# Heads of two tiles at a time, block sums accumulated in PSUM, hid times dt on ScalarE, and the norm's sums by transposes

## The chip, the cores and the metric

The kernel runs on one core of a Trainium2 chip. The metric is the device time of one execution in microseconds. Before the change it is 859.09 us, the median of 3 runs (858.77 to 859.28).

## The reference

One decoder layer in fp32 on x of 2 batches x 256 tokens x 512 channels. Its first part, a state-space block, is where nearly all the time goes:

```
h    = rmsnorm(layernorm(x)) * norm_w
proj = h @ in_proj_w.T                  # gate 8192 | hid 8192, B 1024, C 1024 | dt 128
hBC  = silu(causal_conv(hBC, conv_w) + conv_b)       # 4 taps along the tokens
dt   = softplus(dt + dt_bias);  A = -exp(A_log)
# 128 heads of 64 channels, 8 groups of 16 heads; chunks of 128 tokens
L    = exp(segsum(A * dt))                           # decay between tokens
y    = ((C B^T) * L) @ (hid * dt)  + state of the chunk before + Dp * hid
yg   = y * silu(gate)
y    = yg * rsqrt(mean over each group of 1024 channels of yg^2 + 1e-5) * gnorm_w
x    = x + layernorm(x) + y @ out_proj_w.T
```

Then follow a product of fake-quantised rows with a fake-quantised context, and a feed-forward part with a low-rank mix of experts; they are the last 60 us or so.

## The kernel before

The 512 tokens lie side by side (T = 512, two batches of S = 256). The 8192 channels are 64 tiles of 128 channels, two heads each. Eight tiles make a group g (0 to 7). The main loop (L979 to L1074) is a software pipeline over steps: step s begins tile z, goes on with z1 (begun a step before) and ends z2 (two before). A group has nine steps, q = 0 to 8: eight tiles and, at q = 4, the B and C channels of the next group ("State"; the last group has none and so has eight steps). The order of the instructions on TensorE, VectorE, ScalarE and GpSimd is the order of the program text; only the DMA queue on SP is ordered by the scheduler.

A step does the following.

- `begin(z)` projects the tile's gate and hid rows. In group 0 and for the first tile of group 1 ("plain") this is eight products of 512 columns. Later a scheme with seven block products instead of eight is used (Strassen's): a block product is two matmuls of 128x128 by 256 columns. `begin` issues four of them, `complete` three. In between, ScalarE copies one product to SBUF (`copy_first`, L387), VectorE forms sums (`sum_begun`, L395 to L397), and after `complete` VectorE adds what is saved (`sum_complete`, L410, L411). `sum_weights` on GpSimd forms the sums of the weights (L352 to L355) for the next step's tile.
- `start_conv` and `Conv.finish`: the first tap with the bias on ScalarE (L313), three taps on VectorE (L318), silu on ScalarE (L321). `gates` makes silu of the gate.
- `decayed` and `weighted` for both heads: a scan on VectorE (L493), two multiplies on ScalarE (L497), and GpSimd's product with C B^T (`inner`), called mT (L503).
- `seventh`: the output projection of the group before, also in seven blocks m1 to m7 of eight matmuls with 256 columns (L637). Which block runs at which q is in `usual`; m2 and m4 are split over two steps (q = 2 and 3, q = 8 and 0). Before them GpSimd forms sums of yw and wo (`usual_sums`, L584 to L612). m6, at q = 4, needs the sums of L590 and L604, made at q = 3.
- `heads(z2)`: eight matmuls of 64 weight columns for the tile's two heads, which fill two halves of the array (L513). `gated`: VectorE adds the skip term and multiplies by the gate (L525, L528), ScalarE squares (L533) and scales (L535), GpSimd adds up the squares (L534).
- `by_tokens(z1)`: four transposes of hid on TensorE into the bank "misc" (L477), and on VectorE hid times dt for the heads (L481, called hc).
- `norm(outs[g - 1])` at q = 2: four matmuls of the summed squares with a column of ones (L542), VectorE (L546), then the inverse root on GpSimd (L41 to L51).

On TensorE the order within a step is: `begin`, C B^T or the norm where they are due, block, heads, transposes, `complete`. A matmul in fp32 is two records in the trace, a transpose one. PSUM's eight banks: "py" (heads), "misc", "seed", "po" (blocks), and four for the projection, as two buffers of two banks.

Of the kernel before, what the change touches and what calls it, by code (L numbers as in the profile page):

```python
# [14 lines left out]
NB = 2  # L15
# [39 lines left out]
def kernel(  # L55
# [40 lines left out]
    ramp = const.tile([P, P], F32, name="ramp")  # L96
# [36 lines left out]
    nc.vector.tensor_tensor_scan(ramp[:], ones[:], ones[:], 0.0, ALU.mult, ALU.add)  # L133
    rowno = ps_misc.tile([P, P], F32, tag="misc", name="rowno")
    nc.tensor.matmul(rowno[:], ramp[0:1, :], ones[0:1, :], start=True, stop=True)
    nc.vector.tensor_tensor(ident[:], rowno[:], ramp[:], ALU.is_equal)
# [5 lines left out]
    with ExitStack() as first:  # L142
# [22 lines left out]
        for b in range(NB):  # L165
# [5 lines left out]
            if b == 0:  # L171
                halves = [
                    ps.tile([P, 2, S], F32, tag=tag, name=f"pt_0_{tag}")[:]
                    for ps, tag in ((ps_misc, "misc"), (ps_y, "py"))
                ]
            else:
                halves = [
                    ps_proj.tile([P, 2, T], F32, tag="xy", name=f"pt_1_{h}")[:, 0, :].rearrange("p (k s) -> p k s", k=2)
                    for h in range(2)
                ]  # L180
# [115 lines left out]
    def multiply(out, w, h):  # L296
        for k in range(KD // 2):
            nc.tensor.matmul(out, w[:, k, :], h[:, k, :], start=(k == 0), stop=(k == KD // 2 - 1))  # L298
# [59 lines left out]
    def begin(z):  # L358

        if isinstance(z, State) and z.plain:  # L360

            c = ps_out.tile([P, T], F32, tag="po", name=f"c_{z.g}")
            if z.g == 0:
                b = ps_misc.tile([P, T], F32, tag="misc", name="b_0")
                z.xy = [b[:], c[:]]
            else:
                xy = ps_proj.tile([P, 2, T], F32, tag="xy", name=f"b_{z.g}")
                z.xy = [xy[:, 0, :], c[:]]
        else:
            xy = ps_proj.tile([P, 2, T], F32, tag="xy", name=f"xy_{z.name}")  # L370
            z.xy = [xy[:, n, :] for n in range(2)]
            z.flat = xy[:].rearrange("p n s -> p (n s)")
        if z.plain:
            for n in range(2):
                project(z.xy[n], z.w[:, n])
            return
        z.halves = [z.xy[n][:, half] for n in range(2) for half in (slice(0, S), slice(S, T))]
        x0, x1, y0, y1 = z.halves
        multiply(x0, z.a11, h00)
        multiply(x1, z.s2, t2)  # L380
        multiply(y0, z.s1, t1)
        multiply(y1, z.s3, t3)

    def copy_first(z):
        if not z.plain:
            z.u = pool.tile([P, 2, S], F32, tag="u", name=f"u_{z.name}")
            nc.scalar.copy(z.u[:, 0], z.halves[0])  # L387

    def sum_begun(z):
        if not z.plain:  # L390
            z.v = pool.tile([P, 2, S], F32, tag="v", name=f"v_{z.name}", bufs=1)
            _, x1, _, y1 = z.halves
            u0, u1 = z.u[:, 0], z.u[:, 1]
            y = by_batch(z.xy[1])
            nc.vector.tensor_tensor(u1, x1, u0, ALU.subtract)  # L395
            nc.vector.tensor_tensor(z.v[:], y, z.u[:, 1:2].to_broadcast([P, 2, S]), ALU.subtract)
            nc.vector.tensor_tensor(u1, z.v[:, 0], y1, ALU.add)  # L397

    def complete(z):
        if not z.plain:  # L400
            _, x1, y0, y1 = z.halves
            multiply(x1, z.a12, h10)
            multiply(y0, z.s4, h11)
            multiply(y1, z.a22, t4)

    def sum_complete(z):
        if not z.plain:
            x1 = z.halves[1]
            y = by_batch(z.xy[1])
            nc.vector.tensor_tensor(x1, x1, z.u[:, 0], ALU.add)  # L410
            nc.vector.tensor_tensor(y, y, z.v[:], ALU.add)  # L411

    def hid_of(z):
        return by_batch(z.xy[0] if z.plain else z.flat[:, S : S + T])

    def start_conv(z):
        if isinstance(z, Tile):
            z.hid = pool.tile([P, T], F32, tag="hid", name=f"hid_{z.c}", bufs=2)
            z.convs = [Conv(z.hid[:], [hid_of(z)], cw[:, z.c], z.c, f"h_{z.c}")]
# [3 lines left out]
        z.convs = [Conv(z.sT[0][:], [hid_of(z)], cw[:, 64 + g], 64 + g, f"b_{g}")]  # L423
        if z.plain:
            pvs, w = [by_batch(z.xy[1])], cw[:, 72 + g]
        else:

            pvs, w = [a.unsqueeze(1) for a in (z.halves[3], z.u[:, 1])], ncw[:, g]
        z.convs.append(Conv(z.sT[1][:], pvs, w, 72 + g, f"c_{g}"))

    def gates(z, half):
        if half == 0:
            z.gate = pool.tile([P, T], F32, tag="gate", name=f"gate_{z.c}", bufs=2)
        cols = slice(half * S, (half + 1) * S)
        if not z.plain:

            nc.scalar.activation(z.gate[:, cols], (z.halves[3], z.u[:, 1])[half], AF.Silu, scale=-1.0)
# [34 lines left out]
    def by_tokens(z):  # L472

        c = z.c
        pht = ps_misc.tile([P, NT, 2, HD], F32, tag="misc", name=f"pht_{c}")
        for t in range(NT):
            nc.tensor.transpose(  # L477
                pht[:, t].rearrange("p h d -> p (h d)"), z.hid[:, t * P : (t + 1) * P], ident[:]
            )
        z.hc = pool.tile([P, NT, 2, HD], F32, tag="hc", name=f"hc_{c}", bufs=2)  # L480
        nc.vector.tensor_tensor(  # L481
            z.hc[:],
            pht[:],
            dt[:, :, 2 * c : 2 * c + 2].unsqueeze(3).to_broadcast([P, NT, 2, HD]),
            ALU.mult,
        )

    def decayed(z, n):
# [3 lines left out]
        lT = pool.tile([P, NT + NB, P], F32, tag="lT", name=f"lT_{z.c}_{n}", bufs=4)  # L492
# [7 lines left out]
    def weighted(z, n, inner):  # L500

        m = pool.tile([P, NT + NB, P], F32, tag="mT", name=f"mT_{z.c}_{n}", bufs=4)
# [3 lines left out]
    def heads(z):  # L506

        z.py = ps_y.tile([P, T], F32, tag="py", name=f"py_{z.c}")
# [12 lines left out]
    def gated(z, sqsum, yw):  # L521
# [9 lines left out]
        else:  # L531
            sq = pool.tile([P, T], F32, tag="sq", name=f"sq_{c}", bufs=1)
# [4 lines left out]
    def norm(o):  # L537

        g = o.g
        pss = ps_misc.tile([P, NT], F32, tag="misc", name=f"pss_{g}")  # L540
        for t in range(NT):
            nc.tensor.matmul(  # L542
                pss[:, t : t + 1], o.sqsum[:, t * P : (t + 1) * P], ones[:, 0:1], start=True, stop=True
            )
        var = small.tile([P, NT], F32, tag="var", name=f"var_{g}")
        nc.vector.tensor_scalar(var[:], pss[:], 1.0 / (GJ * P), 1e-5, ALU.mult, ALU.add)  # L546
# [206 lines left out]
    class Rows:  # L753
# [17 lines left out]
        def scaled(self, name, scale):  # L771
# [10 lines left out]
            self.x = pool.tile([P, D], F32, tag="hid", name=f"x_{name}_{t}", bufs=2)  # L782
# [118 lines left out]
    def experts(lo):  # L901
# [21 lines left out]
        for t in range(NT):  # L923
            pf = rows[t].pf
            out_t = pool.tile([P, D], F32, tag="lT", name=f"out_{t}", bufs=4)
# [10 lines left out]
    def finish(z):  # L936
        g, j = divmod(z.c, GJ)
        o = outs[g]
        heads(z)
        if j == 0:  # L940
            o.sqsum = pool.tile([P, T], F32, tag="sqsum", name=f"sqsum_{g}", bufs=1)
        if j % 2 == 0:
            new_yw(o)
        gated(z, o.sqsum, o.yw[-1][:, j % 2, :])
# [26 lines left out]

    sum_inputs()
# [6 lines left out]
    for s, (g, q, z) in enumerate(order):  # L979
# [8 lines left out]
        if z1:  # L988
            sum_complete(z1)
# [7 lines left out]
        if z1:  # L997
            start_conv(z1)
        if tile1:
# [14 lines left out]
        if q == 2 and 0 < g < NG:  # L1014
            norm(outs[g - 1])
        if z:
            sum_begun(z)
        if z1 and not tile1:
            z1.convs[1].finish()
            state = z1  # L1020
        for o, turn in ((outs[g] if g < NG else None, q - GT), (outs[g - 1], q)):
# [21 lines left out]
        o = outs[g - 1]  # L1043
        if not going and 0 <= o.g < g and not o.plain and q in turns[o.g]:
            going.append(seventh(o, *turns[o.g][q]))
# [17 lines left out]
        if isinstance(z2, Tile):  # L1063
            finish(z2)
        if tile1:
            by_tokens(z1)
        if z:
            complete(z)
        if 2 <= s < 2 + 2 + NT:
# [125 lines left out]
```

## Time and profile before

| | |
|---|---|
| median of 3 runs | 859.09 us (858.77 to 859.28) |
| the profiled execution | 858.99 us, span 856.5 us |
| granted TensorE clock | 0.998 |
| busy: TensorE, VectorE, GpSimd, ScalarE | 849.2, 725.5, 655.5, 365.1 us |
| DMA | 116.21 MB, mean 136 GB/s |
| TensorE and GpSimd from 319.93 to 417.52 us (nine steps) | 97.47 and 86.63 of 97.59 us |
| mean of one: L481, L396, L410, L411 (VectorE) | 681, 692, 430, 699 ns |
| mean of one: L387, L497, L535 (ScalarE) | 372, 395, 706 ns |
| mean of one: L503, L534 (GpSimd) | 1819, 1283 ns |

The span is from the first to the last instruction of the profiled execution; what lies around it (2.5 us here) is in the run's time but not in the span. A row of the timeline has its start, its length, the engine, the line, what is written from what, the shape, and how many instructions are merged in it. Matmuls overlap in their pipeline, so their lengths add up to more than the time that passes; from the start of one row to the start of the next is what passes.

### The profile page before, as it was taken

The page shows a single profiled execution, that of the slowest core. Times are in us where ns is not written, and L with a number is a line of the kernel's source. Part 1 is how long each engine was busy: PE and PEld are TensorE (multiplying, and loading weights), DVE is VectorE, ACT ScalarE, POOL GpSimd, SP SyncE. Part 2 cuts the span into 40 slices and gives each one's busy share as a digit, 9 for nine tenths or more (in the row PEclk, how much of TensorE's full clock was granted, in tenths as well). Part 3 has the DMA queues.
Part 4 walks back from the last instruction along what each step waited for, and adds up shares of the span by engine and source line. Part 5 has one row for each costly group of instructions (what it writes and reads, how often), then busy time and mean ns, then how long its engine had stood idle before and what let it go on. Part 6 is the DMA issues. An engine that isn't in the chain of part 4 may idle for free.

```text
span 856.5 us, 13149 instructions
## 1 busy us (share of the span) xinstructions
PE 849.2 (99%) x4432; PEld 655.2 (76%) x4432; DVE 725.5 (85%) x1146; ACT 365.1 (43%) x791; POOL 655.5 (77%) x674
## 2 busy tenths in 40 slices
PE   9999999999999999999999999999999999999998
PEld 6444588888888888888888888888888888885453
DVE  5788699899989899899989899899899898995663
ACT  2444554444544544435443444434443444443220
POOL 2156789988899779997899789997899789973210
PEclk9999999999999999999999999999999999999999
DMA  5774463237542483235632374235433363323001
GB/s 173 221 292 129 128 184 126 81 110 225 171 122 86 124 269 125 86 123 183 212 123 86 116 223 130 75 111 189 161 122 91 118 222 106 123 86 124 0 1 49
DMA packets 54419, 116.21 MB, mean 136 GB/s; under 512 B 7217, under 2 KB 7473, under 8 KB 54354
## 3 DMA queue, kind: packets, MB, share of 16 engines
q1 hardware_dynamic: 54354, 115.39, 42.0%
q8 instruction: 35, 0.57, 0.3%
q14 instruction: 30, 0.25, 0.1%
HBM read 111.83 MB, written 3.54 MB: 135 GB/s over the span
## 4 chain that ended last, share of the span: by engine, by line
PE 90%; DVE 6%; issue 1%; DMA 1%; ACT 1%; SPq 0%; ACTq 0%
PE xy L298 35%; PE m L637 18%; PE py L513 10%; PE xy L294 7%; PE xy_bc L298 4%; PE pht L477 4%; PE po L694 3%; DVE conv_h L318 2%; PE pf L803 2%; PE pq L803 2%; DVE lT L493 1%; PE pcb L446 1%; PE b L294 1%; PE c L294 1%; PE pss L542 1%
## 5 line engine op out<-in xcount | busy, mean ns | idle before, releaser
L503 POOL TENSOR_TENSOR mT<-lT,inner 128x768 f32<-128x768 f32 x128 | 232.7, 1819 | 91.6 <-ACT lT L497 89.0
L493 DVE TENSOR_TENSOR_SCAN lT<-dec,seed 128x512 f32<-128x512 f32 x128 | 154.9, 1211 | 0.0
L637 PE MATMUL m<-wo,yw 128*128 128x256 f32 x672 | 154.6, 380 | 0.0
L318 DVE SCALAR_TENSOR_TENSOR conv_h<-xy,cw,conv_h 128x510 f32<-128x510 f32 (+2 forms) x192 | 143.0, 745 | 13.0 <-ACT gate L439 4.9
L637 PEld LDWEIGHTS m<-wo,yw 128*128 128x128 f32 x672 | 125.9, 190 | 16.8 <-POOL wo L604 0.7
L497 ACT ACTIVATE lT<-dec,lT 128x128 f32<-128x128 f32 x256 | 88.6, 395 | 115.4 <-DVE lT L493 109.5
L298 PE MATMUL xy<-hT,w 128*128 128x256 f32 x440 | 114.1, 382 | 0.5
L298 PE MATMUL xy<-hs,w 128*128 128x256 f32 x440 | 112.9, 379 | 0.0
L298 PE MATMUL xy<-hs,ws 128*128 128x256 f32 x440 | 103.9, 379 | 0.0
L513 PE MATMUL py<-mT,hc 128*64 128x256 f32 (+1 forms) x1024 | 97.3, 332 | 0.0
L534 POOL TENSOR_TENSOR sqsum<-sqsum,sq 128x512 f32<-128x512 f32 x56 | 71.9, 1283 | 33.0 <-ACT sq L533 33.0
L513 PEld LDWEIGHTS py<-mT,hc 128*64 128x64 f32 x1024 | 63.4, 136 | 42.3 <-issue 19.8
L298 PEld LDWEIGHTS xy<-hs,w 128*128 128x128 f32 x440 | 83.6, 190 | 11.4
L298 PEld LDWEIGHTS xy<-hs,ws 128*128 128x128 f32 x440 | 83.6, 190 | 11.4
L298 PEld LDWEIGHTS xy<-hT,w 128*128 128x128 f32 x440 | 79.2, 190 | 11.0 <-DVE u L397 1.5
L313 ACT ACTIVATE conv_h<-xy,cb,cw 128x512 f32<-128x512 f32 x64 | 49.6, 775 | 62.9 <-DVE xy L411 62.6
L533 ACT ACTIVATE sq<-y 128x512 f32<-128x512 f32 x56 | 35.3, 630 | 95.0 <-DVE y L528 95.0
L525 DVE SCALAR_TENSOR_TENSOR py<-hid,dsk,py 128x512 f32<-128x512 f32 x64 | 47.8, 746 | 19.1 <-PE py L513 18.5
L294 PE MATMUL xy<-hT,w 128*128 128x512 f32 x144 | 63.4, 593 | 0.0
L298 PE MATMUL xy<-hT,ws 128*128 128x256 f32 x220 | 56.5, 379 | 0.0
L321 ACT ACTIVATE hid<-conv_h 128x512 f32<-128x512 f32 x64 | 40.2, 628 | 29.5 <-DVE conv_h L318 29.1
L294 PEld LDWEIGHTS xy<-hT,w 128*128 128x128 f32 x144 | 26.7, 190 | 30.4 <-issue 29.4
(230 smaller groups left out, 1395.0 us busy)
## 6 DMA issues: line engine op xcount, KB each, us to landing
dec<-decays SPq DMA_DIRECT2D x128, 384.0 KB, 3.5
w<-in_in_w SPq DMA_DIRECT2D x128, 256.0 KB, 3.0
wo<-in_out_w SPq DMA_DIRECT2D x16, 1024.0 KB, 6.0
w_bc<-in_in_w SPq DMA_DIRECT2D x16, 256.0 KB, 3.2
kvin<-in_ctx_kv SPq DMA_DIRECT2D x4, 512.0 KB, 4.0
kvq<-kvin SPq DMA_DIRECT2D x4, 512.0 KB, 5.3
kv<-kvq SPq DMA_DIRECT2D x4, 512.0 KB, 3.6
acc<-in_x SPq DMA_DIRECT2D x4, 256.0 KB, 3.5
```

Of the source, the lines that this page charges most:

```text
L294: nc.tensor.matmul(pp, w[:, k, :], hT[:, k, :], start=(k == 0), stop=(k == KD - 1))
L298: nc.tensor.matmul(out, w[:, k, :], h[:, k, :], start=(k == 0), stop=(k == KD // 2 - 1))
L313: nc.scalar.activation(a, pv, AF.Identity, bias=cb[:, c : c + 1], scale=w[:, 3:4])
L318: nc.vector.scalar_tensor_tensor(a[:, :, d:], pv[:, :, : S - d], self.w[:, 3 - d : 4 - d], a[:, :, d:], ALU.mult, ALU.add)
L321: nc.scalar.activation(self.dst, self.a[:], AF.Silu)
L493: nc.vector.tensor_tensor_scan(lT[:, 0:NT, :].rearrange("p t i -> p (t i)"), dec[:, 0:T], seed[:], 0.0, ALU.mult, ALU.add)
L497: nc.scalar.mul(lT[:, NT + b, :], dec[:, T + b * P : T + (b + 1) * P], lT[:, 2 * b, P - 1 : P])
L503: nc.gpsimd.tensor_tensor(m[:], z.lT[n][:], inner[:], ALU.mult)
L513: nc.tensor.matmul(z.py[n * HD : (n + 1) * HD, b * S + s * P : (b + 1) * S], z.hc[:, 2 * b + s, n, :], z.mT[n][:, part, :], start=(s == 0) ...
L525: nc.vector.scalar_tensor_tensor(py[:], hid[:], dsk[:, c : c + 1], py[:], ALU.mult, ALU.add)
L534: nc.gpsimd.tensor_tensor(sqsum[:], sqsum[:], sq[:], ALU.add)
L637: nc.tensor.matmul(o.po[:, t, :], lhs[k][:, t * P : (t + 1) * P], rhs[k], start=(k == 0), stop=(k == GJ // 2 - 1))
```

## The change

Heads. `finish` takes a list: tiles are gathered until there are two (or one, in group 0 and at q = 0 and 1), then the heads of both are issued one after the other and after that both are gated. An even tile's result goes to bank "py", an odd one's to "misc". The transposes of z1 come after `complete` and go to whichever of the two banks is given (`free`). hid and gate get three buffers, mT six, sq two; lT three instead of four.

hid times dt. At the next step's start, ahead of `gates` and `copy_first`, ScalarE multiplies the transposed values by dt, for each token tile and head: eight instructions of 128x64 instead of VectorE's one of 128x512.

Block sums. The two projection banks of a tile are allocated apart ("x" and "y"). `begin` writes four block products in another order and place, `copy_first` copies two of them, VectorE makes four sums of 256 columns, partly in PSUM itself, and `complete` adds its three block products to what is in PSUM by accumulation (only the first product that writes a bank clears it). `sum_complete` is gone.

Norm. Four transposes of the summed squares into "py", then a VectorE reduction along the free axis; `norm` is called after `sum_begun`.

Also, the ramp that makes the identity shares its buffer, and the condition that starts a block of `seventh` is written otherwise, with the same blocks at the same steps.

```diff
-    def multiply(out, w, h):
+    def multiply(out, w, h, clear=False):
         for k in range(KD // 2):
-            nc.tensor.matmul(out, w[:, k, :], h[:, k, :], start=(k == 0), stop=(k == KD // 2 - 1))
+            nc.tensor.matmul(out, w[:, k, :], h[:, k, :], start=clear and k == 0, stop=(k == KD // 2 - 1), skip_group_check=True)
...
-        z.halves = [z.xy[n][:, half] for n in range(2) for half in (slice(0, S), slice(S, T))]
-        x0, x1, y0, y1 = z.halves
-        multiply(x0, z.a11, h00)
-        multiply(x1, z.s2, t2)
-        multiply(y0, z.s1, t1)
-        multiply(y1, z.s3, t3)
+        z.h0, z.h1, z.g0, z.all = (z.xy[n][:, half] for n in range(2) for half in (slice(0, S), slice(S, T)))
+        multiply(z.g0, z.s3, t3, clear=True)
+        multiply(z.all, z.s2, t2)
+        multiply(z.h0, z.a11, h00, clear=True)
+        multiply(z.h1, z.s1, t1)
...
-            z.u = pool.tile([P, 2, S], F32, tag="u", name=f"u_{z.name}")
-            nc.scalar.copy(z.u[:, 0], z.halves[0])
+            z.first = pool.tile([P, 2, S], F32, tag="first", name=f"first_{z.name}", bufs=1)
+            nc.scalar.copy(z.first[:, 1], z.g0)
+            nc.scalar.copy(z.first[:, 0], z.h0)
...
-            nc.vector.tensor_tensor(u1, x1, u0, ALU.subtract)
-            nc.vector.tensor_tensor(z.v[:], y, z.u[:, 1:2].to_broadcast([P, 2, S]), ALU.subtract)
-            nc.vector.tensor_tensor(u1, z.v[:, 0], y1, ALU.add)
+            z.g1 = pool.tile([P, S], F32, tag="g1", name=f"g1_{z.name}")[:]
+            u = z.first[:, 0]
+            nc.vector.tensor_tensor(u, z.all, u, ALU.subtract)
+            nc.vector.tensor_tensor(z.h1, z.h1, u, ALU.subtract)
+            nc.vector.tensor_tensor(z.g1, z.h1, z.first[:, 1], ALU.add)
+            nc.vector.tensor_tensor(z.g0, z.g0, u, ALU.subtract)
...
-            multiply(x1, z.a12, h10)
-            multiply(y0, z.s4, h11)
-            multiply(y1, z.a22, t4)
-
-    def sum_complete(z):
-        if not z.plain:
-            x1 = z.halves[1]
-            y = by_batch(z.xy[1])
-            nc.vector.tensor_tensor(x1, x1, z.u[:, 0], ALU.add)
-            nc.vector.tensor_tensor(y, y, z.v[:], ALU.add)
+            multiply(z.h0, z.a12, h10)
+            multiply(z.h1, z.s4, h11)
+            multiply(z.g0, z.a22, t4)
...
-    def by_tokens(z):
+    def by_tokens(z, bank):
...
+        ps, tag = ((ps_misc, "misc"), (ps_y, "py"))[bank]
+        pht = ps.tile([P, NT, 2, HD], F32, tag=tag, name=f"pht_{c}")
...
+    def times_dt(z):
+        c, pht = z.c, z.pht
         z.hc = pool.tile([P, NT, 2, HD], F32, tag="hc", name=f"hc_{c}", bufs=2)
-        nc.vector.tensor_tensor(
-            z.hc[:],
-            pht[:],
-            dt[:, :, 2 * c : 2 * c + 2].unsqueeze(3).to_broadcast([P, NT, 2, HD]),
-            ALU.mult,
-        )
+        for t in range(NT):
+            for n in range(2):
+                h = 2 * c + n
+                nc.scalar.mul(z.hc[:, t, n], pht[:, t, n], dt[:, t, h : h + 1])
...
-            nc.tensor.matmul(
-                pss[:, t : t + 1], o.sqsum[:, t * P : (t + 1) * P], ones[:, 0:1], start=True, stop=True
-            )
+            nc.tensor.transpose(pss[:, t, :], o.sqsum[:, t * P : (t + 1) * P], ident[:])
         var = small.tile([P, NT], F32, tag="var", name=f"var_{g}")
-        nc.vector.tensor_scalar(var[:], pss[:], 1.0 / (GJ * P), 1e-5, ALU.mult, ALU.add)
+        nc.vector.tensor_reduce(var[:], pss[:], AX.X, ALU.add)
+        nc.vector.tensor_scalar(var[:], var[:], 1.0 / (GJ * P), 1e-5, ALU.mult, ALU.add)
...
-    def finish(z):
+    def finish(pair):
+
+        for z in pair:
+            heads(z)
+        for z in pair:
...
-        if z1:
-            sum_complete(z1)
...
+        if isinstance(z2, Tile):
+            times_dt(z2)
...
-        if not going and 0 <= o.g < g and not o.plain and q in turns[o.g]:
-            going.append(seventh(o, *turns[o.g][q]))
+        for n in (1, 2):
+            turn = q + (n - 1) * GT
+            if 0 <= g - n < NG - 1 and turn in turns[g - n]:
+                going.append(seventh(outs[g - n], *turns[g - n][turn]))
...
-            finish(z2)
-        if tile1:
-            by_tokens(z1)
+            pair.append(z2)
+
+        done = len(pair) == 2 or len(pair) == 1 and (q < 2 or g == 0)
+        free = 0
+        if done:
+            free = 1 - len(pair) % 2 * (1 - pair[0].c % 2)
+            finish(pair)
+            pair = []
         if z:
             complete(z)
+        if tile1:
+            by_tokens(z1, free)
```

## Prediction before the run

> **What bounds the kernel now.** I read the page's busy times, then the chain that ended last, then the timeline of TensorE, start to start, and last VectorE, ScalarE and GpSimd in the same window.
>
> ```profile
> PE 849.2 (99%) x4432; PEld 655.2 (76%) x4432; DVE 725.5 (85%) x1146; ACT 365.1 (43%) x791; POOL 655.5 (77%) x674
> ...
> PE 90%; DVE 6%; issue 1%; DMA 1%; ACT 1%; SPq 0%; ACTq 0%
> ```
>
> TensorE is in use all the time and carries 90% of the chain. But a busy TensorE can still stand between instructions, so I read its timeline by the distance from one row's start to the next row's start.
>
> ```profile
> 410.59 0.66 PE L477 MATMUL pht<-ident,hid 128*128 128x128 f32 x4
> 411.37 1.13 PE L298 MATMUL xy<-hT,w 128*128 128x256 f32 x4
> 412.34 1.03 PE L298 MATMUL xy<-hT,ws 128*128 128x256 f32 x4
> 413.20 1.03 PE L298 MATMUL xy<-hs,w 128*128 128x256 f32 x4
> ...
> 417.52 0.95 PE L542 MATMUL pss<-ones,sqsum 128*128 128x1 f32 x8
> 418.33 1.97 PE L637 MATMUL m<-wo,yw 128*128 128x256 f32 x8
> 420.23 1.52 PE L513 MATMUL py<-mT,hc 128*64 128x256 f32 x16
> 421.69 0.66 PE L477 MATMUL pht<-ident,hid 128*128 128x128 f32 x4
> 422.18 1.03 PE L298 MATMUL xy<-hT,w 128*128 128x256 f32 x4
> 423.04 1.03 PE L298 MATMUL xy<-hT,ws 128*128 128x256 f32 x4
> ```
>
> Four records of a 256-column product take 0.86 to 0.87 us (412.34 to 413.20), so 0.216 us each; that is the flow. Against it: (a) eight L637 records should take 1.73 us and take 1.90 (418.33 to 420.23): 0.08 after the one-column products of L542, 0.09 on entering the heads. (b) The heads (L513) take 1.46 us. Their eight matmuls are two records each, and two heads flow side by side, so 1.30 us is flow; 0.05 is lost behind the first pair and 0.09 on leaving. (c) The transposes take 0.49 us, against 4 x 0.109 = 0.44 when nothing precedes them. So a run of heads with transposes behind it costs 0.09 + 0.05 + 0.09 + 0.06 = 0.29 us beside its flow. With a full product behind it (the next rows) that product's first four records take 0.97 instead of 0.87: 0.34 us.
>
> ```profile
> 355.56 1.52 PE L513 MATMUL py<-mT,hc 128*64 128x256 f32 x16
> 357.01 1.13 PE L298 MATMUL xy<-hT,w 128*128 128x256 f32 x4
> 357.98 1.03 PE L298 MATMUL xy<-hT,ws 128*128 128x256 f32 x4
> ```
>
> (d) At 410.59 the transposes are followed only at 411.37, 0.78 later: TensorE waits for VectorE's u (L397). This pause of 0.39 us comes four times (118, 216, 313 and 411 us), always in q = 1 of a group in which VectorE also quantises the context (L269, L270). (e) The last tight place is GpSimd's:
>
> ```profile
> 419.11 1.82 POOL L503 TENSOR_TENSOR mT<-lT,inner 128x768 f32<-128x768 f32 x1
> ...
> 436.28 2.49 POOL L604 TENSOR_TENSOR wo<-wo,t 128x512 f32<-128x512 f32 x2
> ```
>
> ```profile
> 438.04 3.65 PE L637 MATMUL m<-wo,yw 128*128 128x256 f32 x16
> ```
>
> Between these GpSimd has no gap. The block m6 starts at 438.04 and needs the second L604 result, done at 438.77, from its third product on, at 438.9: nothing is to spare. If TensorE comes earlier there, it waits.
>
> **The change, part by part.** Times are within one step of the loop, t = 0 at TensorE's first projection product.
>
> Pairs of heads. The instruction order of the changed kernel has 43 runs of heads instead of 64: group 0 singly, then per group three pairs and two singles. The transposes move behind the products that complete the projection. Before: 56 runs with transposes behind at 0.29 and 8 with a product behind at 0.34, 19.3 us with unrounded sums (0.295, 0.343). After: 7 and 36, 14.4 us. Gain 4.9 us, all on TensorE. What is delayed: the first tile of a pair comes one step later; its buffers (hid, gate three, mT six) cover that, and its py, pht and hc buffers are read at least a step before they are wanted again.
>
> Norm. Eight one-column records (0.81 + 0.08 us) become four transposes (0.44): 0.45 us, seven times on the path, 3.2 us. The Trainium skill speaks against it: "TensorE: Matmul & The Clock Gate", Part 4: PE-mode transpose, gives about 275 ns for a transpose within a kernel; four would be 1.10 us, and the seven norms would lose 1.5 us. The row here has 0.109 us from start to start for just this form, so I take the gain. VectorE gets a reduction of 128x512 (nearest row L481, 0.68) ahead of L546, so the scale comes about 0.5 us later. In the last norm TensorE gains 0.45 while add_out starts 0.4 later, with other products between: I count -0.2 (from -0.5 to +0.4).
>
> Block sums in PSUM. VectorE drops L396, L410 and L411 (0.69 + 0.43 + 0.70) and issues two more of 0.42: -0.97 us for each of 61 tiles. With hc (0.68 x 64) gone and the reductions added, VectorE goes from 725 to about 628 us. TensorE's products stay as many. The only part of this on the path is (d): the sums are then done at about t = 5.8 in q = 1 (context 0.9, scan 1.2, convolution 2.3, three sums 1.35), and the completing products want them at 6.91 + 1.55 = 8.4. Gain 4 x 0.39 = 1.5 us. Without this cover it stays at nothing.
>
> hid times dt on ScalarE, and one more copy (0.37). The trace has no 128x64 multiply from PSUM.
>
> ```profile
> L497 ACT ACTIVATE lT<-dec,lT 128x128 f32<-128x128 f32 x256 | 88.6, 395 | 115.4 <-DVE lT L493 109.5 <-DMA dec<-decays 5.9
> ...
> L387 ACT COPY u<-xy 128x256 f32<-128x256 f32 x55 | 20.5, 372 | 52.7 <-PE xy L298 52.6
> ...
> L194 ACT ACTIVATE hT<-pt,nw 128x256 f32<-128x256 f32 x2 | 0.8, 471 | 0.1
> ```
>
> Two multiplies follow each other at 0.31 us with 128 columns (L497) and at 0.37 with 256 (L194, which reads PSUM). At the 0.83 ns per column between the 512- and 256-column copies, 64 columns give 0.25 and 0.21; I take 0.24, bounds 0.21 and 0.31. Eight are 1.9 us a tile; ScalarE goes from 365 to about 510 us. They stand ahead of the two copies and of L497 in ScalarE's queue, and for those wait VectorE's sums, the completing products and GpSimd's mT. In most steps this is hidden: the second copy cannot start before t = 3.7 (417.77 - 414.07 in the trace: all four products have to end), and convolution 0.6, eight multiplies to 2.5, gate and first copy to 3.25 are through by then. The copy ends at 4.07, three sums at 5.5. The completing products want them at 5.6 in q = 2 (projection 3.46, norm 0.44, half a block 1.73), at 6.7 in q = 0, at 6.9 in q = 4 and 6, later elsewhere. So cover is thin, and three places get a wait:
> - m6 in q = 4. From q = 2's start TensorE needs 8.65 + 11.15 + 3.46 = 23.3 us to m6 (before: 438.04 - 414.07 = 23.97). GpSimd's stretch of 19.66 us (419.11 to 438.77) starts at 4.8, not 5.04, because mT waits for L497, that for the second copy; perhaps 0.2 goes to the later norm. It ends at 24.5 to 24.7; the third product wants it at 24.15. Wait 0.3 to 0.5 and 0.1 to restart: 0.5 us in 6 groups, 3.0 us (0 to 4).
> - q = 0 with the context's Relu (L267, 1.23 us) at the head of ScalarE's queue, after the pair of q = 8, whose second y waits until ScalarE has read the first (one buffer): ScalarE starts at 0.5 and ends the copies at 5.5; sums at 6.9 against 6.7: 0.2 in 4 groups, 0.8 us (0 to 3).
> - q = 6, behind q = 5, where VectorE has the six sums of conv_c (3.3 us) ahead of the pair: ScalarE comes to the next convolution at 2.5, VectorE ends it at 5.65, sums at 7.0 against 6.9: with the restart 0.15 in 7 groups, 1.0 us (0 to 3).
>
> Ramp and identity in one buffer, lT with three buffers (the scan that reuses one comes at least half a step after its reader), and the list of blocks, which starts the same blocks in the same steps: nothing.
>
> Sum: -4.9 - 3.2 - 1.5 - 0.2 + 3.0 + 0.8 + 1.0 = -5.0 us. Span 856.5 to 851.5. The profiled execution took 859.0 with 2.5 us around the span, its median is 859.1: forecast 854.0 us.
>
> **Rivals.**
> No wait arises. GpSimd's stretch starts earlier by what TensorE gains, and the sums are ready. For it: every wait above is under half a microsecond. Against it: at 438.04 nothing is to spare. 854.0 - 4.8 = 849.2 us.
>
> The gains are eaten. The three waits at their upper ends, 4 + 3 + 3, give 859.2 us: no change. For it: cover of 0.1 to 0.2 us in q = 0, 2 and 6 is within what I can place. Against it: two of them need ScalarE late although it is idle 40% of the time.
>
> Slower: the eight multiplies set the pace. The place is ScalarE's queue in q = 2 and q = 0. Up to 0.30 us each they end in time for the copy at 3.7; beyond, each 0.1 us delays copies, L497 and mT by 0.8, which m6 pays 6 times, q = 0 four to seven times: some 9 us. At 0.36 us each the gain is gone; at 0.45, 854 + 13 = 867 us. For it: L194 takes 0.47 alone. Against it: even with 256 columns two follow each other at 0.37.
>
> **How the numbers follow.** Forecast 0.53 (851 to 857); no wait 0.20; eaten 0.13; slower 0.14. The range leaves out the lower half of "no wait" and most of "slower": 848.5 to 861. A change of 0.2% (1.7 us) is about what can be told from none: faster, under 857.4, 0.75; within, 0.11; slower, 0.14.
>
> **What would show it.** 43 runs of heads, and pairs that take 2.75 us from start to start (2.60 + 0.05 + 0.09); the norm's transposes 0.44; no pause in q = 1; the row of the multiplies near 0.31 us each, the eight in about 2 us; VectorE near 630 us, ScalarE near 510. Waits of TensorE for GpSimd's wo in q = 4. Wrong would be: pauses ahead of the completing products in most steps (ScalarE's order), or heads that wait for hc or mT.

## The result, and the profile after

The changed kernel takes 852.25 us, the median of 5 runs (851.84 to 852.51), against 859.09 before: a ratio of 0.9918, 95% interval 0.9905 to 0.9932. The forecast was 854.0 us, its likeliest range 851 to 857. The profiled execution took 852.51 us, its span is 850.7 us at a granted clock of 0.998 (before: 858.99 and 856.5).

The page of the changed kernel, busy times and then the chain that ended last:

```profile
PE 842.1 (99%) x4400; PEld 652.7 (77%) x4400; DVE 629.8 (74%) x1029; ACT 476.0 (56%) x1364; POOL 654.6 (77%) x674
...
PE 83%; POOL 10%; DVE 3%; issue 2%; DMA 1%; ACT 1%; SPq 0%; POOLq 0%; DVEq 0%; ACTq 0%
```

VectorE lost 95.7 us of work, ScalarE gained 110.9, and the time went down by 6.8. TensorE's share of the chain fell from 90 to 83% and GpSimd, which had none, now holds 10%: the chain now runs through GpSimd's stretch ahead of the forecast wait. (The wait itself is 0.44 us in six groups; the 10% is all the work that the chain passes through, not time lost.) The timeline of TensorE after the change, from q = 2 to q = 4 of group 4 (start, length, engine, line, what from what, shape, count):

```profile
415.35 0.60 PE L537 MATMUL pss<-ident,sqsum 128*128 128x128 f32 x4
415.79 1.89 PE L631 MATMUL m<-wo,yw 128*128 128x256 f32 x8
417.53 1.10 PE L298 MATMUL x<-hT,w 128*128 128x256 f32 x4
418.46 1.03 PE L298 MATMUL x<-hT,ws 128*128 128x256 f32 x4
...
425.90 2.82 PE L508 MATMUL py<-mT,hc 128*64 128x256 f32 x32
428.65 1.13 PE L298 MATMUL x<-hT,w 128*128 128x256 f32 x4
429.62 1.03 PE L298 MATMUL x<-hT,ws 128*128 128x256 f32 x4
...
435.24 4.06 PE L631 MATMUL m<-wo,yw 128*128 128x256 f32 x16
439.14 1.03 PE L298 MATMUL x_bc<-hT,w_bc 128*128 128x256 f32 x4
```

The norm's transposes take 0.44 us (415.35 to 415.79). A pair of heads takes 2.75 (425.90 to 428.65), the product behind it 0.97 instead of 0.87. The block m6 takes 3.90 (435.24 to 439.14), where sixteen records that flow take 3.46: 0.44 us is lost. In q = 2 the completing product takes 0.93 instead of 0.87 (417.53 to 418.46), a hesitation of 0.07 that was not forecast. GpSimd at that time, and ScalarE's multiplies in the page's groups (busy us, mean ns of one | idle before):

```profile
431.14 2.79 POOL L584 TENSOR_TENSOR yw<-s,yw 128x256 f32<-128x256 f32 x4
433.89 2.50 POOL L598 TENSOR_TENSOR wo<-wo,t 128x512 f32<-128x512 f32 x2
436.34 1.83 POOL L497 TENSOR_TENSOR mT<-lT,inner 128x768 f32<-128x768 f32 x1
```

```profile
L480 ACT ACTIVATE hc<-pht,dt 128x64 f32<-128x64 f32 x512 | 111.3, 330 | 7.8 <-PE pht L469 7.8
```

The second wo of L598 is ready at 436.4, 1.15 us after m6 began. The eight multiplies of a tile, 330 ns each, overlap: they start 0.197 us apart and take 1.74 us from the first start to the last end.

By stages, after minus before, a stage lasting from one norm to the next: the three that begin in groups 4 to 6 (usual groups, below) are 0.65 to 0.67 us shorter each (97.17 to 96.52 in the last of them), the three that end with a pause of q = 1 in the kernel before 0.9 to 1.07 (97.59 to 96.52 in the third), the one before the last norm 1.59, and the tail behind it is nearly even. A usual group is -0.69 (heads) - 0.45 (norm) + 0.44 (m6) + 0.07 (q = 2) = -0.63.

### The profile page after: what moved, and what is told of

The parts are those of the page before. It is cut to its first block, busy times and chain, and to the rows that moved or that the text cites. A ratio compares the mean times of both kernels' runs of the same rounds, so it can differ in the third digit from the quotient of the medians.

```text
span 850.7 us, 13551 instructions
## 1 busy us (share of the span) xinstructions
PE 842.1 (99%) x4400; PEld 652.7 (77%) x4400; DVE 629.8 (74%) x1029; ACT 476.0 (56%) x1364; POOL 654.6 (77%) x674
## 4 chain that ended last, share of the span: by engine, by line
PE 83%; POOL 10%; DVE 3%; issue 2%; DMA 1%; ACT 1%; SPq 0%; POOLq 0%; DVEq 0%; ACTq 0%
PE x L298 20%; PE m L631 17%; PE y L298 14%; PE py L508 8%; PE x L292 4%; PE y L292 4%; PE po L688 3%; PE pht L469 3%; POOL mT L497 2%; POOL yw L584 2%; POOL wo L598 2%; PE pf L797 2%; PE pq L797 2%; POOL t L593 1%; PE x_bc L298 1%
## 5 line engine op out<-in xcount | busy, mean ns | idle before, releaser
L318 DVE SCALAR_TENSOR_TENSOR conv_h<-x,cw,conv_h 128x510 f32<-128x510 f32 (+2 forms) x192 | 142.8, 744 | 37.3 <-ACT conv_h L313 32.4
L298 PE MATMUL x<-hT,w 128*128 128x256 f32 x440 | 116.9, 388 | 0.5 <-DVE g L397 0.5
L480 ACT ACTIVATE hc<-pht,dt 128x64 f32<-128x64 f32 x512 | 111.3, 330 | 7.8 <-PE pht L469 7.8
L298 PE MATMUL y<-hs,w 128*128 128x256 f32 x440 | 112.1, 379 | 0.0
L298 PEld LDWEIGHTS x<-hT,w 128*128 128x128 f32 x440 | 80.3, 190 | 17.0 <-issue 4.6
L298 PEld LDWEIGHTS y<-hs,w 128*128 128x128 f32 x440 | 79.8, 190 | 8.8
L313 ACT ACTIVATE conv_h<-x,cb,cw 128x512 f32<-128x512 f32 x64 | 48.9, 765 | 19.1 <-PE x L298 19.1
L298 PE MATMUL x<-hs,ws 128*128 128x256 f32 x220 | 56.5, 379 | 0.0
L298 PE MATMUL x<-hT,ws 128*128 128x256 f32 x220 | 56.5, 379 | 0.0
L298 PE MATMUL y<-hs,ws 128*128 128x256 f32 x220 | 56.4, 379 | 0.0
L523 DVE TENSOR_TENSOR y<-py,gate 128x512 f32<-128x512 f32 x64 | 44.2, 691 | 15.1 <-ACT yw L530 13.6
```

The source lines that it names most:

```text
L298: nc.tensor.matmul(out, w[:, k, :], h[:, k, :], start=clear and k == 0, stop=(k == KD // 2 - 1), skip_group_check=True)
L313: nc.scalar.activation(a, pv, AF.Identity, bias=cb[:, c : c + 1], scale=w[:, 3:4])
L318: nc.vector.scalar_tensor_tensor(a[:, :, d:], pv[:, :, : S - d], self.w[:, 3 - d : 4 - d], a[:, :, d:], ALU.mult, ALU.add)
L480: nc.scalar.mul(z.hc[:, t, n], pht[:, t, n], dt[:, t, h : h + 1])
```

## The experiments

The first seven runs are the changed kernel with one part edited each; the last five combine edits. Medians of 4 to 11 runs. The kernel before took 859.2 to 859.6 us beside them and 859.1 beside the changed kernel, so a difference is sure to about 0.5 us.

| run | us | ratio to before | against |
|---|---|---|---|
| heads singly | 861.99 | 1.0027 [1.0016, 1.0038] | changed +9.7 |
| norm by ones | 852.71 | 0.9921 [0.9908, 0.9933] | changed +0.5 |
| hc on VectorE | 853.62 | 0.9932 [0.9919, 0.9944] | changed +1.4 |
| m5 and m6 exchanged | 851.53 | 0.9907 [0.9892, 0.9922] | changed -0.7 |
| old block sums | 913.08 | 1.0619 [1.0593, 1.0644] | changed +60.8 |
| Newton step on VectorE | 849.80 | 0.9896 [0.9882, 0.9909] | changed -2.4 |
| multiplies twice | 880.63 | 1.0245 [1.0230, 1.0260] | changed +28.4 |
| Newton step on VectorE, ones | 852.73 | 0.9927 [0.9914, 0.9941] | Newton alone +2.9 |
| singly, ones | 860.45 | 1.0015 [1.0006, 1.0024] | singly alone -1.5 |
| old sums, hc on VectorE | 866.82 | 1.0080 [1.0065, 1.0095] | hc on VectorE +13.2 |
| old sums, hc on VectorE, singly, ones | 867.84 | 1.0097 [1.0080, 1.0114] | singly, ones +7.4 |
| Newton step, transposes first | 869.08 | 1.0108 [1.0091, 1.0125] | Newton alone +19.3 |

### The norm and the wait at m6

Norm by ones:

```diff
-            nc.tensor.transpose(pss[:, t, :], o.sqsum[:, t * P : (t + 1) * P], ident[:])
+            nc.tensor.matmul(pss[:, t : t + 1], o.sqsum[:, t * P : (t + 1) * P], ones[:, 0:1], start=True, stop=True)
```

> From the changed kernel the norm's sums alone go back to products with a column of ones. Theory (the wait at m6 stands behind the norm in the same stretch and ends when GpSimd ends, whatever TensorE does): the eight one-column records take 0.89 us instead of 0.44 in the trace, but in six groups the wait of 0.44 us at m6 shrinks by as much, and only the last group pays in full: 0.2 to 1.0 us slower than the changed kernel, 852.5 to 853.3 us, and the wait at m6 is gone. Rival (the sum of the prediction, where each norm is on the path by itself): 7 x 0.45 = 3.2 us slower, about 855.4 us.

The Newton step (the last four instructions of the inverse root, L48 to L51) on VectorE, and the same with ones:

```diff
-        newton(nc.gpsimd, small, o.rstd[:], power(...), var[:], NT, f"g{g}")
+        r0 = power(nc, small, var[:], NT, f"g{g}")
+        step = lambda engine: newton(engine, small, o.rstd[:], r0, var[:], NT, f"g{g}")
+        if o.plain:
+            step(nc.gpsimd)
+        else:
+            ends_of.append(lambda: step(nc.vector))
...
-            ends_of.pop()()
+            ends_of.pop(0)()
```

> From the changed kernel the four small instructions of the Newton step (L48 to L51, about 0.97 us of GpSimd's stretch ahead of m6) go to VectorE at the beginning of the next step, except in the last group. The stretch gets 0.97 us shorter, and so does all that GpSimd does behind it, s3 of q = 5 included. Theory (TensorE waits at m6 for the length of this stretch): the wait of 0.44 us is gone in six groups and none takes its place: 6 x 0.44 = 2.6 us faster than the changed kernel, about 849.6 us. Rival (TensorE is as far ahead of VectorE or ScalarE as of GpSimd, so the next engine stops it): 0 to 1 us faster, and a wait for another engine shows in q = 3 to q = 6.

> The edit of the run with the Newton step on VectorE together with the norm's sums as products with a column of ones. Theory (the ones cost only 0.5 us in the changed kernel because the wait at m6 swallowed the rest; without that wait they cost their full length): 7 x 0.45 = 3.2 us slower than the run with the Newton step on VectorE alone, and about as fast as the run with ones alone, 852.8 us. Rival (the norm's length is hidden for another reason): within 1 us of the run with the Newton step alone.

The same edit costs 0.5 us at most while TensorE waits at m6 (the kernel before was as much slower beside that run, and the usual stages with ones are even 0.07 us shorter, 96.45 against 96.52), and 2.9 us once that wait is gone. Both theories held. TensorE in the run with the Newton step on VectorE, and then GpSimd there:

```profile
433.88 3.62 PE L636 MATMUL m<-wo,yw 128*128 128x256 f32 x16
437.33 1.03 PE L298 MATMUL x_bc<-hT,w_bc 128*128 128x256 f32 x4
```

```profile
431.41 2.50 POOL L603 TENSOR_TENSOR wo<-wo,t 128x512 f32<-128x512 f32 x2
433.86 1.82 POOL L497 TENSOR_TENSOR mT<-lT,inner 128x768 f32<-128x768 f32 x1
```

m6 flows (3.45 us), because wo is ready when it begins. From norm to norm a usual group takes 96.08 instead of 96.52 us, six times, and the span is 848.0 instead of 850.7 us. This is the fastest kernel here. Its ratio's interval and the changed kernel's still overlap by a little (0.9882 to 0.9909 against 0.9905 to 0.9932); that the gain is real is read from the six stages. With ones added, its usual groups take 96.45.

### Where a wait goes when the block moves

```diff
-    usual = {1: (0, 0), 2: (1, 1), 4: (2, 0), 5: (3, 0), ...}
+    usual = {1: (0, 0), 2: (1, 1), 4: (3, 0), 5: (2, 0), ...}
-        early = o.g == NG - 2
+        early = True
```

> From the changed kernel the two blocks m5 and m6 of the output product exchange their places in the list, so that the block that needs GpSimd's last result (yw of the second half, the second wo) comes one step later. Theory (the wait of 0.44 us at m6 is on the path in six groups and nothing else is late behind it): 6 x 0.44 = 2.6 us faster than the changed kernel, about 849.6 us; one more add on VectorE and one copy per group are hidden. Rival (the stall is only moved: the next product on GpSimd's chain, s3 of q = 5, ends at 29.67 us after q = 2's start, and q = 5 begins at 29.9 before, at 29.4 if TensorE gains 0.44): the wait comes back there as 0.2 to 0.4 us, and the gain is 0 to 1.3 us, about 851.5 us.

The gain is the rival's, 0.7 us, but not from the rival's place. m6's wait is gone, and the products at the beginning of q = 5 start on time. TensorE stops in q = 6, ahead of the completing products; VectorE's rows are below TensorE's:

```profile
456.90 3.62 PE L631 MATMUL m<-wo,yw 128*128 128x256 f32 x16
460.59 1.10 PE L298 MATMUL x<-hT,w 128*128 128x256 f32 x4
461.53 1.03 PE L298 MATMUL x<-hT,ws 128*128 128x256 f32 x4
```

```profile
450.18 1.19 DVE L663 TENSOR_TENSOR ou<-ou,ou 128x512 f32<-128x512 f32 x1
451.30 0.74 DVE L520 SCALAR_TENSOR_TENSOR py<-hid,dsk,py 128x512 f32<-128x512 f32 x1
...
460.02 0.42 DVE L397 TENSOR_TENSOR g<-x,first 128x256 f32<-128x256 f32 x1
```

The sixteen records take 3.69 us, the first four of the next product 0.94: 0.23 + 0.07 = 0.30 us in place of 0.44. The six stages with the wait are 0.12 to 0.22 us shorter. The completing product starts 0.15 us after the end of VectorE's sum L397, at 460.44, and so it does in all six groups, as in the one place of the changed kernel where the trace names L397 as what ended TensorE's wait (119.05 us). VectorE is late, as I read the rows, because of the edit itself: with `early` the block m5 is saved by a copy and added behind m6, in q = 5 (L663, 1.19 us), ahead of the gating of the pair, on which the next convolution and the sums of q = 6 follow. In the run with the Newton step on VectorE, which lacks that add, TensorE comes to this block just as soon after the norm (42.27 us, here 42.26) and flows (3.45 us). So the exchange removed GpSimd's wait, and the add that came with it made another; the exchange without the add was not tried.

### Pairs

```diff
-        done = len(pair) == 2 or len(pair) == 1 and (q < 2 or g == 0)
+        done = len(pair) == 1
```

> From the changed kernel the pairs alone are taken out: each tile's heads run by themselves again, with the completing product behind them, 64 runs of heads instead of 43. Theory (a run of heads has a fixed price of 0.34 us beside its flow, and the wait for GpSimd's wo at m6 swallows what is lost just ahead of it): 64 x 0.343 = 22.0 us instead of 14.4 is 7.5 us lost; of this one run in each of six groups (0.34 x 6 = 2.1 us) lies between GpSimd's start and m6 and is swallowed by the wait of 0.44 us there. Slower than the changed kernel by 5.4 us, about 857.7 us, and the wait at m6 falls to about 0.1 us. Rival (the price of a run is small, and the gain came from VectorE's lighter load): under 2 us slower, about 854.

Slower by 9.7, more than either theory gave. TensorE's timeline with single heads, in q = 2:

```profile
419.25 1.89 PE L631 MATMUL m<-wo,yw 128*128 128x256 f32 x8
421.82 1.52 PE L508 MATMUL py<-mT,hc 128*64 128x256 f32 x16 [0.68 <-DVE var L539]
423.27 1.13 PE L298 MATMUL x<-hT,w 128*128 128x256 f32 x4
```

The heads of q = 2 wait for VectorE's reduction L539, which reads the bank py that both use. Three runs of heads more (3 x 0.343 = 1.03), plus 0.75 for this wait, less m6's 0.44 and q = 2's 0.07, make 1.27 us a group, as measured (97.79 against 96.52).

> Single heads and the norm's sums by a column of ones, both at once. In the run with single heads the heads of q = 2 waited 0.75 us in seven groups for VectorE's reduction L539 to read the bank that both use. Theory (the reduction holds this bank; with ones VectorE reads only four columns and lets go at once): the wait of 0.75 us is gone, 0.45 us of products are added: 7 x 0.30 = 2.1 us faster than the run with single heads alone, about 859.9 us. So transposes in the norm would bring a loss unless heads go in pairs. Rival (the transposes bring 0.45 us by themselves): 3.2 us slower than single heads alone, 865.2 us.

Faster than single heads alone by 1.5 us, 0.29 to 0.30 in each usual group; the last group has no such wait and pays for the ones. With ones in both, the pairs are worth 857.85 - 850.85 = 7.0 us of span: 21 runs of heads at 0.33. So the norm's transposes pay only with the pairs, which leave q = 2 without heads.

The order behind the heads, on top of the Newton step on VectorE:

```diff
+        if tile1:
+            by_tokens(z1, free)
         if z:
             complete(z)
-        if tile1:
-            by_tokens(z1, free)
```

> The run with the Newton step on VectorE, and beside that the transposes of hid's values go back between the heads and the completing products. Theory (behind a run of heads transposes lose 0.06 us and a full product 0.10, so a run costs 0.295 instead of 0.343 us): 36 runs x 0.048 = 1.7 us faster than the run with the Newton step alone, about 848.1 us. Rival (the completing products end 0.44 us later in the step, so the next convolution and the copies begin later, and a pause comes in q = 2 or q = 0): same or up to 3 us slower.

Both expectations missed: 19.3 us slower. A pair writes its two y into py and misc, and pht needs one of them: behind a pair the transposes wait until VectorE (L523) has read py. TensorE there:

```profile
433.93 2.82 PE L508 MATMUL py<-mT,hc 128*64 128x256 f32 x32
438.77 1.09 PE L469 MATMUL pht<-ident,hid 128*128 128x128 f32 x4 [2.02 <-DVE y L523]
439.65 1.92 PE L298 MATMUL x<-hT,w 128*128 128x256 f32 x4
441.36 1.44 PE L298 MATMUL x<-hT,ws 128*128 128x256 f32 x4
442.64 1.03 PE L298 MATMUL y<-hs,w 128*128 128x256 f32 x4
```

The completing products, 2.6 us, are the time in which that bank comes free. Their move ahead of the transposes is a condition of the pairs. About 5 of the 19.3 us are a second effect: after three of these pauses TensorE's clock dropped (last section).

### ScalarE's multiplies

hc on VectorE: the eight `nc.scalar.mul` become one `nc.vector.tensor_tensor` at the same place.

> From the changed kernel the multiplication of hid's values by dt alone goes back to VectorE as one instruction of 0.68 us. Theory (both engines have room, so who does it matters only where a sum or a copy is just in time): within 1 us of the changed kernel, 851.3 to 853.3 us; ScalarE's eight multiplies (1.73 us) leave its queue, so the second copy may start no earlier than the products end, but VectorE has 0.68 us more ahead of its sums. Rival (VectorE's relief is what the change lives on): VectorE's sums come 0.7 us later in each step and the pauses of 0.39 us in q = 1 come back, four of them and more in q = 2: 2 to 6 us slower. Third theory (ScalarE's queue delays GpSimd, as the prediction feared): faster by 1 to 2.6 us, because the second copy, L497 and mT come earlier and the wait at m6 shrinks.

1.4 us slower. In the span 0.85 of it is one place, q = 1 of group 1, where VectorE quantises the context while GpSimd works; 0.34 lies at the start of the kernel, where runs differ by as much; usual groups take 0.04 to 0.09 more. So who multiplies matters little, as the first theory had it, a little above its limit.

Multiplies twice: `for t in [*range(NT), *range(NT)]`.

> From the changed kernel ScalarE's eight multiplies of hid's values by dt are issued twice, with the same result: 1.73 us more a tile in ScalarE's queue, as if each took 0.43 us. Theory (the prediction's slower rival: from 0.30 us each on, copies, L491 and mT come late, about 9 us for each 0.1 us): (0.43 - 0.30) / 0.1 x 9 = 12 us slower, about 864 us. In the trace the second copy of q = 2 and q = 3 waits 1.07 us for the products, so 0.7 of the 1.73 us should be left: pauses of TensorE of about 0.7 us in q = 2, and m6 unchanged. Rival (ScalarE is idle 44% of the time, so there is room): under 2 us slower.

28.4 us, more than twice the 12 expected, though the eight more multiplies take only 0.197 us each. There are more places than q = 2's second copy. TensorE in group 5 with the doubled multiplies, then GpSimd and ScalarE:

```profile
524.39 1.10 PE L298 MATMUL x<-hT,w 128*128 128x256 f32 x4 [0.26 <-DVE g L397]
...
530.09 1.03 PE L298 MATMUL x<-hs,ws 128*128 128x256 f32 x4
532.39 0.63 PE L537 MATMUL pss<-ident,sqsum 128*128 128x128 f32 x4 [1.28 <-POOL w L354]
```

```profile
528.29 1.28 POOL L529 TENSOR_TENSOR sqsum<-sqsum,sq 128x512 f32<-128x512 f32 x1
...
528.93 3.37 ACT L480 ACTIVATE hc<-pht,dt 128x64 f32<-128x64 f32 x16
```

The norm begins 1.44 us late. The trace puts this down to GpSimd, but sqsum, which the norm reads, was done 2.8 us earlier. In all seven groups of the loop the norm starts 0.10 us after the end of the last of the sixteen multiplies: they read the values transposed in q = 1 from the bank py, and the norm's transposes write to py. With eight multiplies 1.40 us lie between the two in six of the seven. (The bank as the reason is read from the code and these times; it was not tried by itself.) The completing products of q = 4 lose 0.58 us, waiting for VectorE's sums, those of q = 1 0.33, and the two C B^T products 0.56 together. A usual group is 3.0 us longer, the first three 4.0 to 4.2, and 5.2 are lost before the first norm.

### The block sums

Old sums: four products by themselves, L394 to L396 and two sums behind, one copy on ScalarE fewer. In the three runs with the old sums mT also has five buffers instead of six; GpSimd then waits for TensorE to read mT in two places of one run (3.6 us) and nowhere in the other two.

```diff
-        multiply(z.g0, z.s3, t3, clear=True)
-        multiply(z.all, z.s2, t2)
-        multiply(z.h0, z.a11, h00, clear=True)
-        multiply(z.h1, z.s1, t1)
+        multiply(x0, z.a11, h00)
+        multiply(x1, z.s2, t2)
+        multiply(y0, z.s1, t1)
+        multiply(y1, z.s3, t3)
```

> From the changed kernel the block sums alone go back to the form of the kernel before: four blocks multiplied by themselves, three sums of VectorE between and two behind, one copy of ScalarE fewer. Theory (the accumulation in PSUM is worth what it takes from the path, the pauses of q = 1 in the groups where VectorE also quantises the context): 3 to 4 pauses of about 0.4 us come back, one ScalarE copy less lets the second L491 start earlier: 0.5 to 2 us slower, 852.8 to 854.3 us. Rival one (about 1 us a tile of VectorE's work counts in most steps): VectorE's sums come late in q = 2 and q = 0 as well, 4 us slower or more. Rival two (off the path altogether): within 0.4 us of the changed kernel.

60.8 us, far beyond all three. The list of waits of this run (waiter <- releaser: us in total, times, longest):

```profile
DVE conv_h L317 <- ACT gate L436: 76.8, 46, 2.8
```

In the changed kernel, with the multiplies ahead of the gate as here, the entry is another:

```profile
DVE conv_h L318 <- ACT conv_h L313: 32.4, 38, 2.0
```

With the old sums hid's values lie in halves of the banks x and y, and y also holds half of the gate's. In program order VectorE's convolution stands behind ScalarE's gate, which stands behind the eight multiplies. With the new sums hid's values fill bank x and the gate's are in y and SBUF, and the convolution waits only for its own first term. (The kernel before has the wait for the gate too, without multiplies ahead of it: 4.9 us.) Some 8 of the 61 us are no wait: after five of its long pauses TensorE's clock dropped to half for 3.4 us (last section), and the five runs go from 908.14 us at a granted clock of 0.995 to 915.47 at 0.984.

> The old block sums once more, but with VectorE's one multiplication by dt instead of ScalarE's eight; pairs and the norm's transposes stay. In the run with the old sums alone VectorE's convolution L317 waited 76.8 us in 46 places for ScalarE's gate, which stands behind the eight multiplies and reads the bank y, as the convolution does there; with the new sums the convolution reads the bank x alone and waits only for its own first term. Theory (this coupling, together with the eight multiplies ahead of the gate, made the 61 us): without the eight multiplies nearly all of it goes, and the time is that of the changed kernel plus the old pauses, 853.5 to 857 us. Rival (the old sums are slow by their own length in this order of work): still over 880 us.

Without the eight multiplies ahead of the gate 46 us go, the clock's share with them, so they make most of the 61, and the convolution's wait for the gate is where the trace shows them; that the shared bank is its reason was read from the code, not tried. 13.2 us remain, more than expected. TensorE, q = 2:

```profile
425.47 1.89 PE L642 MATMUL m<-wo,yw 128*128 128x256 f32 x8
428.08 1.10 PE L297 MATMUL xy<-hT,w 128*128 128x256 f32 x4 [0.72 <-DVE u L396]
```

This step of a pair has no heads, and the completing products wait 0.96 us for VectorE's u.

> Old block sums and VectorE's multiplication by dt as in the run before, and also single heads and the norm's sums by a column of ones: nearly the kernel before, but with the transposes of hid's values behind the completing products. In the run with old sums and pairs TensorE waits 0.96 us in q = 2 and 0.78 us in q = 4 for VectorE's u (L396), in steps in which a pair leaves TensorE no heads to run ahead of the completing products. Theory (the heads of each step were the cover of the old sums, 1.5 us in every step; pairs take it from half the steps): with single heads these waits go, and against the run with single heads and ones but new sums (860.45 us) only the pauses of q = 1 are added: 0 to 3 us slower, 860.5 to 863.5 us. Rival (old sums are late in this order of work whatever the heads do): 10 us or more slower than that run, above 870 us.

Neither theory: 7.4 us slower (the move of hc to VectorE, 0.04 to 0.09 in a usual group, is in it). In usual groups the old sums cost 0.32 us with single heads (heads of q = 2 that wait for VectorE to read the norm's sums; the completing products lose nothing) and 1.27 to 1.31 with pairs, so there the cover was the heads. But the pauses of q = 1 are 1.36 and 1.51 us in the two runs, against 0.39 in the kernel before: the transposes no longer stand ahead of the completing products (0.44), hc stands behind the old sums instead of ahead of them on VectorE (0.68). The first belongs to the change, the second to how this run was built; how the rest divides was not tried.

## Why the prediction was right

**Heads, -4.9 us.** Right in mechanism and size: 43 runs, 2.75 us a pair, 0.34 a run. Not seen was that the move of the transposes is not free to choose.

**Norm, -3.2, and m6, +3.0.** Both sizes are right (0.45 us; 0.44 x 6 = 2.7). The step that weighed 275 ns a transpose, from the Trainium skill ("TensorE: Matmul & The Clock Gate", Part 4: PE-mode transpose), against the row's 109 chose well, but the two do not contradict each other: one transpose lasts 272 to 273 ns here too, and four overlap, 109 ns from start to start, in 0.44 us. To multiply a length by four was the mistake. But the sum treats as two terms what is one: m6 waits for GpSimd, so in six groups the 0.45 us gained ahead of it come back as that wait. Alone, the norm is worth 0.5 us at most in this kernel.

**Block sums, -1.5.** The four pauses of q = 1 are gone but for one (0.55 us, group 1). "Without this cover it stays at nothing" was wrong: the saved 0.97 us of VectorE and the separate bank are what the pairs and the multiplies on ScalarE need. As one term of a sum it hid 13 us, and 61 with the multiplies on ScalarE.

**Multiplies on ScalarE.** 0.197 us from start to start, forecast 0.24 between 0.21 and 0.31, so just under the range; ScalarE is busy for 476 us instead of the 510 forecast. The waits in q = 0 and q = 6 (+1.8) did not come; q = 2 lost 0.07 six times instead (0.4). These terms were mis-sized: covers of 0.1 to 0.2 us were beyond what I could place. The slower rival was not met, since 0.197 lies below its limit of 0.30; its slope was too small: the doubled multiplies are as if each took 0.39, some 8 us by that slope, and cost 28.4, in places that it did not name.

**Not foreseen.** In group 0 the heads of an odd tile write to misc and wait 0.62 us once for ScalarE's copy of `inner` (L449); with what else changes there the stage is 0.39 us longer. The start is 0.38 longer, but it moves between 9.3 and 10.5 us over all runs. In sum: 851.5 forecast, -1.8 (q = 0, 6), -0.3 (m6), +0.4 (q = 2), +0.4 and +0.4: 850.6, measured 850.7. That the sum missed the span by only 0.8 us is in part luck, since errors of -2.1 and +1.2 us offset each other. Between span and run 1.8 us lie here instead of 2.5, most of what is left to 854.0.

## What to carry to other kernels

Where an engine waits at the end of another's stretch, gains ahead of that wait are not added to its price: the later of the two ends counts, and shortening the other engine's stretch by 1 us was worth more than four transposes. Price each part of a change with the other parts in place and then without them; a part that saves nothing by itself can carry the rest. When two runs of heads are put together, or an engine's work grows, look at which bank each next writer needs and who reads it last: the heads behind VectorE's reduction, the transposes behind a pair and the norm behind the doubled multiplies all waited for a bank. And an edit made to move a wait can make another: see what else it adds, and where.

## What the runs showed of the hardware

VectorE's small instructions ended with GpSimd's. With the Newton step on VectorE, four columns each; first VectorE, then GpSimd:

```profile
418.35 0.69 DVE L48 TENSOR_TENSOR t_g<-r_g 128x4 f32<-128x4 f32 x1
419.07 0.16 DVE L49 TENSOR_TENSOR t_g<-t_g,var 128x4 f32<-128x4 f32 x1
419.26 0.58 DVE L50 TENSOR_SCALAR t_g<-t_g 128x4 f32<-128x4 f32 x1
419.88 1.18 DVE L51 TENSOR_TENSOR rstd<-r_g,t_g 128x4 f32<-128x4 f32 x1
```

```profile
418.29 0.73 POOL L583 TENSOR_TENSOR s<-yw 128x256 f32<-128x256 f32 x1
419.09 0.73 POOL L584 TENSOR_TENSOR yw<-yw 128x256 f32<-128x256 f32 x1
419.78 2.50 POOL L598 TENSOR_TENSOR t<-wo 128x512 f32<-128x512 f32 x2
```

L48, L50 and L51 end at 419.04, 419.84 and 421.06, GpSimd's at 419.02 and 419.82, and 421.03 is halfway through the next two; L49 fits into the gap between and takes 0.16. The Trainium skill ("SBUF — State Buffer", "SBUF: two separate sides") has a port pair that the two engines share and one holds for a whole instruction, and the rows agree: 2.7 us for what GpSimd does in 1.0. It was still the faster kernel, since VectorE had the room.

TensorE's clock dropped after some pauses of 2.3 us and more. In the run with the transposes first, the table of stretches (start:end, length, busy us of PE, PEld, DVE, ACT and POOL with counts, granted clock, DMA share, GB/s) is:

```profile
423.50:436.70 13.20, 13.20 (x85) 10.94 (x83) 12.08 (x21) 7.23 (x23) 11.64 (x13) 1.00 0.39 130
436.70:438.70 2.00, 0.05 (x2) 0.00 (x0) 1.97 (x4) 0.74 (x3) 2.00 (x2) 1.00 0.09 25
438.70:442.30 3.60, 3.53 (x11) 3.03 (x12) 2.95 (x5) 2.45 (x4) 3.60 (x6) 0.53 0.31 100
```

For 3.4 us records of 256 columns come every 0.43 instead of 0.216 us; against the run with the Newton step alone stages with this lose 3.9 to 4.2 us, those without it 2.2. From the start of one matmul to the start of the next, six pauses of this run are 2.3 to 2.6 us long, and it followed three of them. In the run with the old block sums it followed five of eleven of 2.5 to 2.8 us, and with doubled multiplies not the one of 2.6. No pause up to 2.2 us led to it in any run. The Trainium skill ("TensorE: Matmul & The Clock Gate", Part 1) names a free-running window of about 3.4 us for the clock gate, which fits that it strikes only sometimes.
